# A product with two weight matrices, its seven-product form applied a second time and its weights read through a ring

## The chip, the cores and the metric

The kernel runs on one core of one Trainium2 chip. The metric is the device time of one execution in microseconds (us); lower is better. The core has a matrix engine (TensorE, in profiles PE, its weight loads PEld), three engines for element-wise work (VectorE or DVE, ScalarE or ACT, GpSimd or POOL), and SyncE (SP), which here issues all DMA transfers. Each engine runs its own instructions in program order and waits on semaphores for the others. Matmul results land in PSUM, in eight banks of 128 x 512 fp32 values[...].

## The reference

For 64 graphs of 256 nodes with 512 features, everything in fp32:

```python
def gcn(x, adj, W, b):
    return einsum('bnm,bmh->bnh', adj, einsum('bnf,fh->bnh', x, W)) + b

# layer 0: three graph convolutions, a residual and a layer norm
h = relu(gcn(x, adj, W1, b1)); h = relu(gcn(h, adj, W2, b2))
x = layernorm(x + gcn(h, adj, W3, b3))
# layer 1: a score for each node, a softmax over the nodes, a residual and a layer norm
q, k = split(x @ Wqk); v = x @ Wv
agg = einsum('bij,bjd->bid', adj, k * mask[:, :, None])
w = mask * einsum('bid,bid->bi', q, agg) / sqrt(512)
x = layernorm(x + softmax(w, axis=1)[:, :, None] * v)
```

The kernel forms M = Wq Wk^T once. Then the score of a node is the inner product of its row of x1 M with its row of A (x1 mask), where x1 is the result of layer 0. So layer 1 needs the product of x1 with two weight matrices, [Wv | M]: 256 x 512 times 512 x 1024 for each graph. The change is about this product.

## The kernel before

The graphs are worked in 32 pairs. The order on each engine is the order in which the code issues instructions (`manual_schedule`). For each pair there are three generators: `front` (F: layer 0 up to the third support), `back` (B: the last aggregation, the norm, the gather A x1, then `attention`, the double product with the scores) and `finish` (E: softmax, residual, norm, store). `run` interleaves front of pair i, back of pair i-1 and finish of pair i-2 by a string of letters written out by hand: `START` for the first round, `ORDER` for the 31 rounds after it, `END` for the round that has no front.

Products with 2 x 2 blocks are done with seven block products in place of eight. The helper `seven` issues them in the order 1, 7, 6, 2, 5, 3, 4 on three PSUM banks x, v and y, with a `yield` after each. Product 1 goes to x, is copied to SBUF by ScalarE (t1), then 6 is added in x and copied (u), then 5 is added and copied (q), then 3 is added and x holds block C12. Product 7 goes to v; VectorE forms C22 = v + q; then 4 is added in v and VectorE forms C21 = v + u. Product 2 goes to y and VectorE forms C11 = y + t1. So product 6 waits for the copy of t1, 5 for that of u, 3 for that of q, and 4 for VectorE's C22. The sums of the left operand are made by `a_sums` (four instructions, on GpSimd in the steady part), those of the right one by `b_sums`.

`front` runs three `support`s (four matmuls of 256 columns for each of the seven products) and two `aggregate`s (four steps of four matmuls). During the third support it issues on GpSimd the sums of the adjacency (`adj_sums`), the addition of b3 to x (`x<-x,b3b`, four instructions) and the `a_sums` of the next pair's input. `load_x`, `load_xT`, `load_adj` are DMA transfers on SP.

`back` writes the transposed x1 through DRAM (`via`) and back into `x1T`; GpSimd forms the sums S from it. Then `attention(g)` runs for each of the two graphs: seven products of two matmuls with 512 columns each (L451), the node halves and the feature halves of x1 against the blocks of [Wv | M], whose sums `mv` stay in SBUF for the whole kernel. The Wv part gives `v`; the M part is multiplied with the gathered rows `gt` and summed by `score` (VectorE). In the last round (`end`) the attention of the first graph is interleaved with the gather, and that of the second with the finish of the first.

An instruction of the program that multiplies fp32 operands shows as two instructions in the profile.

Of the kernel before, what the change touches and what calls it, by code (L numbers as in the profile page):

```python
# [19 lines left out]
@with_exitstack  # L20
def gcn_then_graph_attention(ctx: ExitStack, tc: tile.TileContext, xT, xN, adjT, mask, W1, b1, W2, b2, W3, b3,
                             WqT, WkT, Wv, out):

# [35 lines left out]
    def add(o, a, b):  # L61
        nc.vector.tensor_tensor(o, a, b, op=OP.add)  # L62
# [34 lines left out]

    def shaped(shape):
        t = tmp()
        return t.rearrange("p (a b) -> p a b", a=shape[1]) if len(shape) == 3 else t  # L100

    def seven(mm, shape, c11, c12, c21, c22, plus=None):

# [87 lines left out]
    eps = const.tile([P, 1], FP, name="eps")  # L191
    nc.vector.memset(eps, EPS)

    mv = {}

    def make_m():

        wq = pool.tile([P, DC, D], FP, name="wqT", tag="r", bufs=1)
        qk = [[wq[:, d] for d in range(DC)],
              [pool.tile([P, D], FP, name="wkT", tag="T", bufs=4) for _ in range(DC)]]  # L200
        for d in range(DC):
            for t, w in ((qk[0][d], WqT), (qk[1][d], WkT)):
                nc.sync.dma_start(t, w[d * P:(d + 1) * P, :])
        m = [pool.tile([P, 2, D], FP, name="m0", tag="v", bufs=2), const.tile([P, 2, D], FP, name="m1")]
        v0 = const.tile([P, 2, D], FP, name="v0")
        nc.sync.dma_start(v0, Wv[:HD].rearrange("(c p) f -> p c f", p=P))
        v1 = const.tile([P, 2, D], FP, name="v1")
        nc.sync.dma_start(v1, Wv[HD:].rearrange("(c p) f -> p c f", p=P))
        yield
        for f in range(DC):  # L210
            pt = bank((P, D))
            for d in range(DC):
                for j in range(DC):
                    nc.tensor.matmul(pt[:, j * P:(j + 1) * P], lhsT=qk[0][d][:, f * P:(f + 1) * P],  # L214
                                     rhs=qk[1][d][:, j * P:(j + 1) * P], start=(d == 0 and j == 0),
                                     stop=(d == DC - 1), skip_group_check=True)
            nc.scalar.copy(m[f // 2][:, f % 2, :], pt)
            yield
        ts = [const.tile([P, 2, D], FP, name=f"mv_{s}") for s in KEYS]
        b_sums((v0, m[0], v1, m[1]), ts, nc.vector)  # L220
        mv.update({1: v0, 2: v1, 3: m[1], 4: ts[3], 5: ts[0], 6: ts[1], 7: ts[2]})
        yield


    def a_sums(blk, eng=nc.gpsimd):

        S = [pool.tile([P, 2, G, P], FP, name="S", tag="S", bufs=11) for _ in range(4)]
        sub = OP.subtract  # L230

        def first():
            eng.tensor_tensor(S[2], blk(0, 0), blk(1, 0), op=sub)  # L233

        def rest():
            eng.tensor_tensor(S[0], blk(1, 0), blk(1, 1), op=OP.add)
            eng.tensor_tensor(S[1], S[0], blk(0, 0), op=sub)  # L237

        def last():
            eng.tensor_tensor(S[3], blk(0, 1), S[1], op=sub)  # L240
        return {1: blk(0, 0), 2: blk(0, 1), 4: blk(1, 1), 5: S[0], 6: S[1], 7: S[2], 3: S[3]}, first, rest, last

# [23 lines left out]
    def aggregate(C, aT, b):  # L266


        hT = [pool.tile([P, 2, G, N], FP, name="hT", tag="act", bufs=4) for _ in range(2)]
        src, first, rest, last = a_sums(lower_first(hT))  # L270
        for c in (2, 3, 0, 1):
            ps = bank()
# [21 lines left out]
        return {1: blk(0, 0), 2: blk(0, 1), 4: blk(1, 1), 5: S[:, 0], 6: S[:, 1], 7: S[:, 2], 3: S[:, 3]}  # L294

    def t_sums(B):
        Ts = [pool.tile([P, G, HD], FP, name="T", tag="T", bufs=4) for _ in range(4)]
        b_sums((B[0][0], B[0][1], B[1][0], B[1][1]), Ts, nc.gpsimd)
        return Ts

# [46 lines left out]
    def front(i, hT, src, aT):  # L347
        C = yield from support(src, wl[0])
        nxt = load_xT(i + 1) if i + 1 < NPAIR else None
        src, last = yield from aggregate(C, aT, bcol[0])  # L350
        C = yield from support(src, wl[1], last)
        src, last = yield from aggregate(C, aT, bcol[1])
        x = load_x(i)
        steps = support(src, wl[2], last)
        next(steps)
        yield
        next(steps)
        yield
        aS = adj_sums(aT)
        next(steps)  # L360
        yield
        for g in range(G):
            next(steps)
            for h in range(NH):
                padd(x[:, g, h, :], x[:, g, h, :], b3b)
            yield
        nS = None
        if nxt is not None:
            nS, first, rest, last = a_sums(lower_first(nxt))
            first()  # L370
            rest()
            last()
        C = yield from steps
        return C, aS, x, nxt, nS

    def back(i, C, aS, x, end):
# [63 lines left out]
        gt = pool.tile([P, NH, G, D], FP, name="gt", tag="gt", bufs=1)  # L440
        gb = lambda h, j: gt[:, h, :, j * HD:(j + 1) * HD]
        w = small.tile([P, NH, G], FP, name="w", bufs=2)
        vs = [None] * G

        def attention(g):
            b = i * G + g
            v = pool.tile([P, NH, D], FP, name="v", tag="v", bufs=2)

            def mm(n, ps, first):
                for c in range(2):  # L450
                    nc.tensor.matmul(ps, lhsT=src[n][:, c, g], rhs=mv[n][:, c], start=(first and c == 0),  # L451
                                     stop=(c == 1), skip_group_check=True)

            def score(y, h):
                nc.vector.scalar_tensor_tensor(y, y, mask_s[:, h, b:b + 1], gt[:, h, g, :], op0=OP.mult,
                                               op1=OP.mult, accum_out=w[:, h, g:g + 1])

            def c22(ps, t):
                add(t, ps, t)
                score(t, 1)  # L460
            vs[g] = v
            yield from seven(mm, (P, D), lambda y, t: add(v[:, 0, :], y, t), lambda x: score(x, 0),
                             lambda ps, t: add(v[:, 1, :], ps, t), c22)
        gather = adj_times(aS, xmb, Ts, lambda y, t: add(gb(0, 0), y, t), lambda x: nc.scalar.copy(gb(0, 1), x),
                           lambda v, t: add(gb(1, 0), v, t), lambda v, t: add(gb(1, 1), v, t))
        src, first, rest, last = a_sums(x1b, nc.vector if end else nc.gpsimd)
        if end:
            first()
            rest()
            last()  # L470
            one = attention(0)
            for k in "GMGMGMGMGGGMMM":
                next(gather if k == "G" else one)
                yield
            for _ in gather:
                pass
            for _ in one:
                pass
            tail = finish(i, (r, vs, w), [0])
            for _ in attention(1):  # L480
                next(tail, None)
                yield
            for _ in tail:
                pass
            for _ in finish(i, (r, vs, w), [1]):
                pass
            return
        for _ in range(4):
            next(gather)
            yield  # L490
        first()
        rest()
        last()
        yield from gather
        if i + 2 < NPAIR:
            aTs[i + 2] = load_adj(i + 2)
        for g in range(G):
            yield from attention(g)
        return r, vs, w

    def finish(i, prev, gs=range(G)):

        r, vs, w = prev
        n = len(gs)
        sm = softmax_rows(w, gs)
        yield
        s = softmax_cols(sm, gs)
        for k, g in enumerate(gs):
            for h in range(NH):
                nc.vector.scalar_tensor_tensor(vs[g][:, h, :], vs[g][:, h, :], s[:, h, k:k + 1], r[:, g, h, :],  # L510
                                               op0=OP.mult, op1=OP.add)
        yield
        st = small.tile([P, NH, n, 6], FP, name="st")
        mvt = small.tile([P, NH, n, 2], FP, name="mvt")
        for k, g in enumerate(gs):
            for h in range(NH):
                nc.vector.bn_stats(st[:, h, k], vs[g][:, h, :])  # L517
                yield
        for k in range(n):
            for h in range(NH):  # L520
# [2 lines left out]
        yield  # L523
        for k, g in enumerate(gs):
            for h in range(NH):
                nc.scalar.activation(vs[g][:, h, :], vs[g][:, h, :], AF.Identity, scale=rs[:, h, k:k + 1],  # L526
                                     bias=nb[:, h, k:k + 1])
                yield
            nc.sync.dma_start(out[i, :, g * NH * D:(g + 1) * NH * D].rearrange("p (h f) -> p h f", h=NH), vs[g])


    ORDER = ("F E F" + " B F" + " B F E" * 2 + " B B E F E F" + " B F E" + " B F B F F B B F F" +
             " B F B F B F E B B E F F" + " B F E B F E" + " B F E B F E B B F B F B F B" + " B F B F B B F B F B F B")
    START = "F" * 4 + "B" + "F" * 12 + "B" + "F" * 6 + "B FF B FFF B F B F"
    END = "E B B B E" + "B" * 5 + "B E" * 10

    def run(order, **gens):
# [15 lines left out]
    for i in range(NPAIR + 1):  # L553
# [14 lines left out]
        if i < NPAIR:  # L568
            C, aS, x, xTs, xS = res["F"]
            state = (C, aS, x)  # L570


# [33 lines left out]
```

## Time and profile before

| | |
|---|---|
| median of 3 runs | 2839.57 us (2838.18 to 2839.74) |
| the profiled execution | 2837.91 us, its span 2836.1 us |
| granted TensorE clock | 0.998 |
| DMA | 191.00 MB, mean 67 GB/s; SP's queue busy 21.1% of the 16 engines' span |
| chain, largest lines | L254 (support) 41%, L451 (attention) 27%, L275 (aggregate) 16%, L307 (gather and last aggregation) 13% |

A group in the profile reads: line, engine, operation, output<-inputs, shapes, count | busy time in us, mean time of one in ns | idle time of the engine just before these instructions, and who ended it. In a timeline a row begins with start and duration in us and may end with [idle before <-releaser]. Matmuls are pipelined, so the durations of neighbours overlap; the cost of one is the distance of the starts.

### The profile page before, as it was taken

The page shows a single profiled execution, that of the slowest core. Times are in us where ns is not written, and L with a number is a line of the kernel's source. Part 1 is how long each engine was busy: PE and PEld are TensorE (multiplying, and loading weights), DVE is VectorE, ACT ScalarE, POOL GpSimd, SP SyncE. Part 2 cuts the span into 40 slices and gives each one's busy share as a digit, 9 for nine tenths or more (in the row PEclk, how much of TensorE's full clock was granted, in tenths as well). Part 3 has the DMA queues.
Part 4 walks back from the last instruction along what each step waited for, and adds up shares of the span by engine and source line. Part 5 has one row for each costly group of instructions (what it writes and reads, how often), then busy time and mean ns, then how long its engine had stood idle before and what let it go on. Part 6 is the DMA issues. An engine that isn't in the chain of part 4 may idle for free.

```text
span 2836.1 us, 29920 instructions
## 1 busy us (share of the span) xinstructions
PE 2810.0 (99%) x11344; PEld 2191.4 (77%) x11344; DVE 1120.9 (40%) x2326; ACT 945.3 (33%) x1517; POOL 1437.5 (51%) x1122
## 2 busy tenths in 40 slices
PE   9999999999999999999999999999999999999997
PEld 8887778877778877787777788777887777877774
DVE  2444334443344443344433444333444334443335
ACT  2333233332333332333323333323333233333333
POOL 4545455445555455554555554556545455445551
PEclk9999999999999999999999999999999999999999
DMA  4211222211222112222122221122221222211210
GB/s 153 67 60 42 65 80 82 82 42 55 67 82 82 54 44 67 82 82 73 44 63 67 82 82 45 53 67 82 82 64 49 67 67 82 82 45 52 67 60 30
DMA packets 63086, 191.00 MB, mean 67 GB/s; under 512 B 5728, under 2 KB 8928, under 8 KB 54880
## 3 DMA queue, kind: packets, MB, share of 16 engines
q1 hardware_dynamic: 62944, 189.10, 21.1%
q8 instruction: 90, 1.47, 0.2%
q14 instruction: 52, 0.43, 0.1%
HBM read 123.02 MB, written 66.06 MB: 67 GB/s over the span
## 4 chain that ended last, share of the span: by engine, by line
PE 97%; DVE 1%; DMA 1%; ACT 1%; issue 0%; SPq 0%; POOL 0%; ACTq 0%; DVEq 0%; POOLq 0%
PE ps L254 41%; PE ps L451 27%; PE ps L275 16%; PE ps L307 13%; PE ps L214 1%; DMA aT<-in_adjT 0%; PE ps L341 0%; PE ps L326 0%; DMA mask_t<-in_mask 0%; ACT v L526 0%; SPq L149 0%; DVE st L517 0%; POOL tmp L65 0%; DMA out<-v 0%; DVE st L388 0%
## 5 line engine op out<-in xcount | busy, mean ns | idle before, releaser
L254 PE MATMUL ps<-w_T,S 128*128 128x256 f32 x2304 | 546.9, 380 | 2.3 <-POOL S L237 1.5
L254 PEld LDWEIGHTS ps<-w_T,S 128*128 128x128 f32 x2304 | 432.5, 190 | 106.6 <-issue 52.1
L275 PE MATMUL ps<-aT,sup 128*128 128x256 f32 x2048 | 472.7, 379 | 0.0
L275 PEld LDWEIGHTS ps<-aT,sup 128*128 128x128 f32 x2048 | 389.1, 190 | 76.1 <-issue 22.2
L62 DVE TENSOR_TENSOR sup<-ps,tmp 128x512 f32<-128x512 f32 x288 | 198.4, 689 | 526.8 <-PE ps L254 338.4
L451 PE MATMUL ps<-mv_T,S 128*128 128x512 f32 x768 | 361.0, 592 | 0.0
L65 POOL TENSOR_TENSOR tmp<-tmp,x 128x512 f32<-128x512 f32 x96 | 120.5, 1270 | 418.8 <-ACT tmp L126 242.3
L278 ACT ACTIVATE hT<-ps,b 128x512 f32<-128x512 f32 x256 | 175.4, 685 | 377.1 <-PE ps L275 377.1
L62 DVE TENSOR_TENSOR v<-ps,tmp 128x512 f32<-128x512 f32 x128 | 88.5, 692 | 535.5 <-PE ps L451 531.8
L118 ACT COPY tmp<-ps 128x512 f32<-128x512 f32 x224 | 131.3, 586 | 486.3 <-PE ps L254 223.4
L109 ACT COPY tmp<-ps 128x512 f32<-128x512 f32 x224 | 130.7, 583 | 418.0 <-PE ps L254 283.7
L126 ACT COPY tmp<-ps 128x512 f32<-128x512 f32 x224 | 130.7, 583 | 339.0 <-PE ps L254 221.4
L254 PE MATMUL ps<-w,hT 128*128 128x256 f32 x1024 | 241.9, 379 | 0.0
L451 PE MATMUL ps<-v,x1T 128*128 128x512 f32 x512 | 240.6, 592 | 0.0
L254 PEld LDWEIGHTS ps<-w,hT 128*128 128x128 f32 x1024 | 194.5, 190 | 46.3 <-issue 14.8
L451 PEld LDWEIGHTS ps<-mv_T,S 128*128 128x128 f32 x768 | 145.8, 190 | 102.1 <-issue 92.3
L233 POOL TENSOR_TENSOR S<-x1T 128x512 f32<-128x512 f32 x31 | 67.9, 2190 | 275.7 <-DMA x1T<-via 275.7
L307 PE MATMUL ps<-T,aS 128*128 128x256 f32 x768 | 200.3, 383 | 0.3 <-ACT tmp L109 0.3
L451 PEld LDWEIGHTS ps<-v,x1T 128*128 128x128 f32 x512 | 146.2, 290 | 69.3 <-issue 17.7
L233 POOL TENSOR_TENSOR S<-hT 128x512 f32<-128x512 f32 x64 | 81.2, 1269 | 220.5 <-ACT hT L278 220.5
L254 PE MATMUL ps<-w,S 128*128 128x256 f32 x768 | 181.5, 379 | 0.7 <-issue 0.7
L93 POOL TENSOR_TENSOR T<-sup 128x512 f32<-128x512 f32 x32 | 41.0, 1281 | 272.8 <-ACT sup L256 272.8
(109 smaller groups left out, 4179.9 us busy)
## 6 DMA issues: line engine op xcount, KB each, us to landing
x<-in_xN SPq DMA_DIRECT2D x32, 1024.0 KB, 5.7
out<-v SPq DMA_DIRECT2D x64, 512.0 KB, 3.3
xT<-in_xT SPq DMA_DIRECT2D x31, 1024.0 KB, 4.9
via<-tr SPq DMA_DIRECT2D x31, 1024.0 KB, 4.3
x1T<-via SPq DMA_DIRECT2D x124, 256.0 KB, 4.7
aT<-in_adjT SPq DMA_DIRECT2D x32, 512.0 KB, 4.3
w<-in_W SPq DMA_DIRECT2D x9, 256.0 KB, 5.2
xT<-in_xT SPq DMA_DIRECT2D x2, 512.0 KB, 5.1
```

The source lines that it names most:

```text
L62: nc.vector.tensor_tensor(o, a, b, op=OP.add)
L65: nc.gpsimd.tensor_tensor(o, a, b, op=op)
L93: eng.tensor_tensor(Ts[2], B[3], B[1], op=sub)
L109: nc.scalar.copy(t1, x)
L118: nc.scalar.copy(u, x)
L126: nc.scalar.copy(q, x)
L233: eng.tensor_tensor(S[2], blk(0, 0), blk(1, 0), op=sub)
L254: nc.tensor.matmul(ps[:, g], lhsT=src[n][:, c, g], rhs=w[n][:, c], start=(first and g == 0 and c == 0), stop=(g == G - 1 and c == 1), skip ...
L275: nc.tensor.matmul(ps[:, g], lhsT=C[k][c // 2][:, g, (c % 2) * P:(c % 2 + 1) * P], rhs=aT[:, k, g], start=(g == 0 and k == 0), stop=(g == ...
L278: nc.scalar.activation(hT[c // 2][:, c % 2], ps, AF.Relu, bias=b[:, c:c + 1])
L307: nc.tensor.matmul(ps[:, g], lhsT=aS[n][:, g], rhs=mov[n][:, g], start=(first and g == 0), stop=(g == G - 1), skip_group_check=True)
L451: nc.tensor.matmul(ps, lhsT=src[n][:, c, g], rhs=mv[n][:, c], start=(first and c == 0), stop=(c == 1), skip_group_check=True)
```

## The change

The seven block products of the double product (the outer ones) are each again split 2 x 2 and done with seven products (the inner ones). In an inner product the rows are the two graphs of the pair, the contraction is 2 x 128 features and the columns are 2 x 256. That gives 7 x 7 = 49 matmuls of 128 x 128 by 128 x 256 for a pair, where 28 matmuls of 128 x 128 by 128 x 512 stood (two graphs, seven products, two matmuls each).

The outer products run in four groups: a = (1, 2), b = (6, 5), c = (7, 4), d = (3). A step of a, b or c does one inner product for two outer products into one bank; a step of d does one. The groups a and b alternate step by step, then follow c and d. With them come:

- `attention` is one generator for the pair. ScalarE copies three blocks of x1T to Z and VectorE makes the four sums of Z; GpSimd makes the inner sums I in two groups of four. The first inner sums of x1T by GpSimd (S) go.
- Each group collects its blocks in R (a and c in the buffer T, b and d in that of x1T), and VectorE combines the groups with six additions of 1024 columns; d adds to what R holds, three of these additions on GpSimd. Both graphs' scores follow c and d.
- `make_m` forms the 49 weight operands in round 0 and stores them in DRAM (`w_dram`). A ring of 7 SBUF buffers of 256 KB is filled by `fetch`: after each step the transfer for the seventh step after it is issued on SP.
- Fewer buffers: S 11 to 7, hT 4 to 2, T one tile of four parts, v one tile.
- In `front`, the next pair's sums are issued in steps 2 and 5 of the third support, and the additions of b3 in steps 3 and 4. `ORDER` and `START` are rewritten. In the last round only the first steps of a and b stand in the gather, and the finish of both graphs follows the whole product.

```diff
-    mv = {}
+    OUTER = ((1, 2), (6, 5), (7, 4), (3,))
+    INNER = (1, 7, 6, 2, 5, 3, 4)
+    STEPS = "ab" * 7 + "c" * 7 + "d" * 7
+    place = {n: k for k, n in enumerate(n for q in OUTER for n in q)}
+    w_dram = [dram.tile([P, 7, len(q), HD], FP, name=f"mv_{k}", bufs=1) for k, q in enumerate(OUTER)]
...
+    RING = 7
+    ring = {}
+    def fetch(k):
+        if k < NPAIR * len(uses):
+            q, n = uses[k % len(uses)]
+            t = pool.tile([P, 2, HD], FP, name="ring", bufs=RING)
+            nc.sync.dma_start(t[:, :len(OUTER[q])], w_dram[q][:, n])
+            ring[k] = t
...
+        for q, outer in enumerate(OUTER):
+            w = pool.tile([P, 7, len(outer), HD], FP, name="w7", tag="ZI"[q % 2], bufs=1)
+            for k, n in enumerate(outer):
+                blk = [B[n][:, c, j * HD:(j + 1) * HD] for c in range(2) for j in range(2)]
+                for i, b in ((1, blk[0]), (2, blk[2]), (3, blk[3])):
+                    nc.scalar.copy(w[:, at[i], k], b)
+                b_sums(blk, [w[:, at[i], k] for i in (5, 6, 7, 4)], nc.vector)
+                yield
+            nc.sync.dma_start(w_dram[q], w)
+        for k in range(RING):
+            fetch(k)
...
         steps = support(src, wl[2], last)
...
+        for n in range(6):
             next(steps)
-            for h in range(NH):
-                padd(x[:, g, h, :], x[:, g, h, :], b3b)
+            if n == 1:
+                aS = adj_sums(aT)
+            if n == 2 and nxt is not None:
+                nS, first, rest, last = a_sums(lower_first(nxt))
+                first()
+                rest()
+            if n in (3, 4):
+                for h in range(NH):
+                    padd(x[:, n - 3, h, :], x[:, n - 3, h, :], b3b)
+            if n == 5 and nxt is not None:
+                last()
             yield
...
-                    nc.tensor.matmul(ps, lhsT=src[n][:, c, g], rhs=mv[n][:, c], start=(first and c == 0),
-                                     stop=(c == 1), skip_group_check=True)
...
+    def attention(i, x1b, gt, w):
+        Z = pool.tile([P, 7, 4, P], FP, name="Z", tag="Z", bufs=1)
+        I = pool.tile([P, 4, 7, P], FP, name="I", tag="I", bufs=1)
...
+        for n, b in ((1, x1b(0, 0)), (2, x1b(0, 1)), (4, x1b(1, 1))):
+            nc.scalar.copy(z(n), b)
+        for o, a, b, op in ((z(5), x1b(1, 0), x1b(1, 1), OP.add), (z(6), z(5), z(1), sub), (z(7), z(1), x1b(1, 0), sub),
+                            (z(3), z(2), z(6), sub)):
+            nc.vector.tensor_tensor(o, a, b, op=op)
+        for a, b in ((0, 4), (4, 7)):
+            padd(I[:, 2, a:b], Z[:, a:b, 0], Z[:, a:b, 1], sub)
+            padd(I[:, 0, a:b], Z[:, a:b, 1], Z[:, a:b, 3])
+            padd(I[:, 1, a:b], I[:, 0, a:b], Z[:, a:b, 0], sub)
+            padd(I[:, 3, a:b], Z[:, a:b, 2], I[:, 1, a:b], sub)
...
+            def mm(n, ps, first):
+                wt = ring.pop(at[0])
+                for k, o in enumerate(outer):
+                    nc.tensor.matmul(ps[:, k], lhsT=left[n](place[o]), rhs=wt[:, k], start=(first and k == 0),
+                                     stop=(k == len(outer) - 1), skip_group_check=True)
+                fetch(at[0] + RING)
+                at[0] += 1
...
+            if count[k] == 7:
+                if k == "a":
+                    add(v[:, :, 0], flat(R["a"][:, 0]), flat(R["a"][:, 1]))
+                elif k == "b":
+                    U, V = R["b"][:, 0], R["b"][:, 1]
+                    add(U, U, R["a"][:, 0])
+                    add(V, V, U)
+                elif k == "c":
+                    P7, P4 = R["c"][:, 0], R["c"][:, 1]
+                    add(P4, P4, U)
+                    add(v[:, :, 1], flat(P7), flat(P4))
+                    add(P7, P7, V)
+                    score(P7, 1)
+                else:
+                    score(V, 0)
+            yield
+        return v
...
-    ORDER = ("F E F" + " B F" + " B F E" * 2 + " B B E F E F" + " B F E" + " B F B F F B B F F" +
-             " B F B F B F E B B E F F" + " B F E B F E" + " B F E B F E B B F B F B F B" + " B F B F B B F B F B F B")
-    START = "F" * 4 + "B" + "F" * 12 + "B" + "F" * 6 + "B FF B FFF B F B F"
+    ORDER = ("F F E" + " B F" + " B F E" * 2 + " B B E F E F" + " B F E" + " B F B F F B B F F" +
+             " B F B F B F E B B E F F" + " B F E B E" + " B E F E F" + " BB BB BB BB F BB BB BB" +
+             " B B F B B F B F B B F B B F B B F B F B B")
+    START = "F" * 4 + "B" + "F" * 12 + "B" + "F" * 5 + "B F B F B B" + "F B" * 6
...
+    for _ in finish(NPAIR - 1, prev):
+        pass
```

## What the change does to the time, predicted before it was measured

> **What bounds the kernel now.** I read the shares of the engines first, then the chain of waits, then the groups of instructions with shapes kept apart, and last the timelines of one pair of graphs in the steady part, of pair 0 and of the end.
>
> ```profile
> span 2836.1 us, 29920 instructions
> PE 2810.0 (99%) x11344; PEld 2191.4 (77%) x11344; DVE 1120.9 (40%) x2326; ACT 945.3 (33%) x1517; POOL 1437.5 (51%) x1122
> ...
> PE 97%; DVE 1%; DMA 1%; ACT 1%; issue 0%; SPq 0%; POOL 0%; ACTq 0%; DVEq 0%; POOLq 0%
> ...
> L451 PE MATMUL ps<-mv_T,S 128*128 128x512 f32 x768 | 361.0, 592 | 0.0
> ...
> L65 POOL TENSOR_TENSOR x<-x,b3b 128x512 f32<-128x512 f32 x128 | 172.3, 1376 | 0.0
> ```
>
> TensorE is the path: 97% of the chain; apart from its own weight loads, which overlap its matmuls, no engine is over 51%. "Idle before" is zero at L451, so in the steady part nothing makes TensorE wait. A mean of 592 ns is a latency; the cost is the distance of starts, from the timeline of TensorE:
>
> ```profile
> 1075.99 1.89 PE L275 MATMUL ps<-aT,sup 128*128 128x256 f32 x8
> 1077.71 1.88 PE L451 MATMUL ps<-v,x1T 128*128 128x512 f32 x4
> 1079.43 1.89 PE L275 MATMUL ps<-aT,sup 128*128 128x256 f32 x8
> 1081.16 1.88 PE L451 MATMUL ps<-mv_T,S 128*128 128x512 f32 x4
> ```
>
> Four instructions of 512 columns take 1.717 us (429 ns each), eight of 256 take 1.725 us (216 ns each): the cost goes with columns. Pairs start 86.9 us apart (the softmax's reduction at 1032.53 and 1119.43).
>
> Two further views price what the change adds, VectorE and GpSimd in pair 0:
>
> ```profile
> 73.62 1.22 DVE L94 TENSOR_TENSOR mv_T<-m,v 128x1024 f32<-128x1024 f32 x1
> 74.87 2.17 DVE L95 TENSOR_TENSOR mv_T<-m,mv_T 128x1024 f32<-128x1024 f32 x1
> 77.07 2.17 DVE L96 TENSOR_TENSOR mv_T<-v,mv_T 128x1024 f32<-128x1024 f32 x1
> ...
> 74.25 1.71 POOL L93 TENSOR_TENSOR T<-sup 128x512 f32<-128x512 f32 x1 [4.22 <-ACT sup L256]
> 75.92 2.25 POOL L94 TENSOR_TENSOR T<-sup 128x512 f32<-128x512 f32 x1
> ```
>
> An addition of two SBUF operands of 1024 columns takes 1.12 us from start to start alone, but 2.17 us beside a GpSimd one, and that one 2.25 in place of 1.27: each waits until the other has ended. And the end of the kernel, where one step follows another without cover:
>
> ```profile
> 2773.01 1.03 PE L307 MATMUL ps<-T,aS 128*128 128x256 f32 x4
> 2774.71 1.13 PE L307 MATMUL ps<-sup,aS 128*128 128x256 f32 x4 [0.68 <-ACT tmp L126]
> ```
>
> The step at 2773.01 occupies TensorE to 2773.88; the next, on the same bank, starts 0.83 us later. So the copy between two uses of a bank needs 0.83 us of other work.
>
> **What the Trainium skill says.** "SBUF — State Buffer", section "Who interferes with whom": a VectorE instruction with two SBUF inputs contends with a GpSimd instruction that reads SBUF, and the second to issue blocks until the first has finished; the lines above agree (1.12 to 2.17). "TensorE: Matmul & The Clock Gate", table at its head: the queues of ScalarE, VectorE and GpSimd are strict FIFO, so what stands behind a blocked instruction waits too; the trace shows ScalarE's and VectorE's starts in program order. "DMA: Bandwidth & Descriptors", section "Specifications", limits HBM to about 358 GB/s for a core; here 189.10 MB took 21.1% of the span, 316 GB/s while busy, and the measurement counts.
>
> **The change part by part**, for one pair in the steady part.
>
> TensorE. Removed: 2 graphs x 7 products x 2 matmuls, two instructions each, 56 x 429 ns = 24.04 us. Added: 49 matmuls of 256 columns, 98 x 216 = 21.17. Gain 2.85 us a pair; the weights now come from contiguous Z and I (190 ns loads, where x1T took 290), hidden either way under 216. Over 31 pairs -88 us. What counts is whether TensorE stays fed. In totals it does: VectorE gains 3 PSUM additions (0.6), 4 half ones (0.35), 4 sums of Z (0.65) and 6 of 1024 columns (1.12), 12.5 us on 34.3 of 84; ScalarE some 7 us on 29; GpSimd loses 7.2 us (S<-x1T) and gains 8.8 (eight sums of I) and 2.1 (three half additions in d). No engine becomes the bound by its sum; the order decides.
>
> I lay out TensorE's new order from a1 (t = 0, 49.0 us into the pair, the place where the trace has 1079.43). A step of a, b, c takes 0.865, of d 0.43, of the next pair's support or aggregation 1.725. So: a1 0, b1 .87, a7 1.7, b7 2.6, a6 3.46, b6, a2, b2 6.1, aggregation 6.9, a5 8.65 ... b4 13.0, c1 13.8, c7, F0 15.6, c6, c2, F1 19.0, c5, F2, c3 23.4, c4 24.2-25.1, F3, d1 26.8, d7, F4 27.7, d6, d2, F5 30.3, d5 32.0, F6 32.45, d3, d4, next pair at 35.0. (F0 to F6: the seven products of the third support.)
>
> Banks. The tightest uses, a5 to a3 and b5 to b3, have one step of 0.865 between, against 0.83: no stall, at most 0.1.
>
> Early wait (a6). x1T lands at t = -4.4: GpSimd's S<-x1T waits for it to 1075.06. ScalarE has before the three copies to Z a relu (to -3.4) and two normalisations (0.71 each), so Z1 is there at -1.3 and Z2 at -0.6, Z6 on VectorE at -0.6. GpSimd's first I then starts behind Z7 (0), ends at 1.3 (a7 needs it at 1.7), the second waits for VectorE's Z3 and ends at 3.1, the third, which a6 needs, at 4.35. Stall 0.9. Bounds: 0 if the lock is not met (third I at 3.5), 2.0 if the stride of x1T slows the copies as it slows GpSimd (2.19 against 1.27). Behind a6 all of TensorE is queued.
>
> Late wait (F6). F6 adds into the bank that VectorE must first have read for C22 of the same support. That addition stands in VectorE's queue behind the end of c: after c4 (25.1, plus 0.26 to VectorE's start as at L62 now) come one PSUM addition 0.6, three of 1024 columns 3.36, two scores of 0.7, then C11 and C22 of the support 1.3: 32.05 without contention, and F6 loses nothing (0.4 spare). But GpSimd gets d's first half addition at 27.9 (d1's end, then ScalarE's copy), and behind it the last two of x+b3b (1.25 each, two SBUF operands), all ready. Alternating as in pair 0 these three go between the last five SBUF instructions of VectorE: +0.7, +1.25, +1.25, so F6 starts at 35.15. Stall 2.7. Bounds: 0, and 5.8 if all five wait for a GpSimd instruction of 1.25 (x late from its DMA, so all four of x+b3b fall there). Behind F6: d3, d4 and the next pair. Its softmax transposes at 3.45 us need the scores of d, then some 0.5 earlier: nothing added.
>
> SP and DMA. 28 ring transfers of 256 or 128 KB add 6.4 MB to a pair that moves 6.0 now. In the a/b phase one of 256 KB is wanted each 0.865 us (303 GB/s), but each is issued seven steps ahead, 5.2 to 6.9 us; 512 KB land in 3.3 to 4.3 us now, 1024 in 4.9 to 5.7, so 256 KB need about 3.5 (estimate from these). SP's issue is 0.35 to 0.43, under 0.865. Past them must go aT and the second out<-v; before x<-in_xN stand the fetches up to c7, so x comes at t = 16 and lands near 22, used at 23. Price taken: 0; bounds 0 and 2.5 (rival 3).
>
> Fewer buffers (hT, S, T, v at half): their readers end before the reuse in this order (S's last sum waits for F4, 29.4, and isn't needed before the next pair). 0.
>
> End. No support lies beside c and d, both graphs are normalised after all products. From the first product of the second gather (2787.4), by the durations that the end of the trace shows: gather with a1 and b1 10 us (with its waits of 0.97 and 1.16), the other twelve a/b steps 10.4, c 6.9 (seven steps and one 0.83), VectorE's end of c 5.6, d's sums and scores 3.3, softmax 3.7, its application 2.7, statistics and normalisation 6.8, last landing 3.7: 2840.5, +4 us (0 to +12).
>
> Start. 21 copies and 32 additions that build the ring's source lie beside the last support of pair 0, where VectorE and GpSimd meet again: +6 (0 to +15).
>
> Sum against the profiled execution (2837.91 us, 1.8 around its span): 31 x (0.9 + 2.7 - 2.85) = +23, +4, +6: 2871. The median shown is 1.7 above the profiled one: 2873.
>
> **The rivals.** (1) The cover holds (faster): GpSimd's three additions miss the end of c, F6 starts on time. For it: GpSimd is at 51%, and VectorE's own sum leaves 0.4 us. Against it: d1's addition becomes ready in the midst of these sums. 31 x (0.9 - 2.85) + 10 = -50: 2789. It decides once F6's stall is under 1.6 us (2.85 - 0.9 - 10/31). (2) A tie: stalls near 2.5 us in all, as with one GpSimd addition fewer in the way: 2840. (3) The ring is late: at 200 GB/s (aT and out in between) nine fetches need 11.8 us where they have about 11, with the landing some 2.5 us too late, over 31 pairs +78 on the forecast: 2951. Against it: 316 GB/s while busy.
>
> **How the numbers follow.** The lock (2873): 0.52. Rival 1: 0.30; rival 2: 0.08; rival 3: 0.10. Slower by over 0.2% (some 6 us, about what a measurement can tell) 0.62, same 0.08, faster 0.30. The likeliest's own range, stalls of 2.7 to 5.0 us in all with the bounds of start and end, is 2845 to 2925; with rival 1 it reaches down to 2785, and leaves out rival 3 and the ends of the bounds.
>
> **What would show it.** Matmuls from the ring 216 ns apart: the gain. Idle of TensorE before the support's last product, released by VectorE's sup: the late wait, about 2.7 us x 31; before the ring,I products, released by GpSimd: the early one. VectorE's 1024 additions at 2 us rather than 1.22 would prove the lock; at 1.22, and no idle at F6, the forecast is wrong and rival 1 right. Idle released by the ring's DMA is rival 3.

## The result, and the profile after

The changed kernel takes 2929.88 us (median of 4 runs, 2924.93 to 2940.91) against 2839.55 us of the kernel before, measured beside it: 1.0325 times as long, with a 95% interval of 1.0295 to 1.0354. The profiled execution took 2928.85 us. Forecast were 2873 us, with a range of 2785 to 2925: the direction is right, the size is not, and the time lies outside the range.

From the page of the changed kernel: span, engines, the chain of waits by engine, groups of instructions (out<-in, count, busy us, mean ns of one, idle us just before them and what ended it), and the last line a DMA issue with its median time to landing.

```profile
span 2927.0 us, 36919 instructions
...
PE 2776.6 (95%) x12684; PEld 2377.3 (81%) x12684; DVE 1774.5 (61%) x2888; ACT 1167.2 (40%) x1917; POOL 1756.3 (60%) x1350
...
PE 74%; DVE 11%; POOL 5%; ACT 4%; issue 3%; DMA 2%; SPq 0%; ACTq 0%; DVEq 0%
...
L520 PE MATMUL ps<-ring,I 128*128 128x256 f32 x1792 | 455.3, 385 | 32.7 <-POOL I L68 31.5
...
L65 DVE TENSOR_TENSOR R<-R 128x1024 f32<-128x1024 f32 x128 | 232.3, 1815 | 9.2 <-DVE R L65 0.5
L68 POOL TENSOR_TENSOR x<-x,b3b 128x512 f32<-128x512 f32 x128 | 207.5, 1642 | 15.4 <-DMA x<-in_xN 9.7
...
L289 PE MATMUL ps<-w_T,hT 128*128 128x256 f32 x512 | 141.1, 424 | 78.0 <-DVE sup L65 78.0
...
ring<-mv SPq DMA_DIRECT2D x672, 256.0 KB, 3.2
```

TensorE's share of the chain fell from 97% to 74%. Most of its idle time in the steady part stands at two places. 78.0 us come before the product with w_T and hT that waits for VectorE's sup: the support's last product, F6. 32.7 us come before a product of the ring with I, a6, which waits for GpSimd's third sum of I. A ring transfer lands in 3.2 us, and none of TensorE's groups waits for one.

One steady pair on TensorE's timeline (start us, duration us, operation, in brackets the idle before it and what ended it):

```profile
1118.76 1.99 PE L520 MATMUL ps<-ring,I 128*128 128x256 f32 x8
1121.77 1.99 PE L520 MATMUL ps<-ring,I 128*128 128x256 f32 x8 [1.02 <-POOL I L68]
...
1150.61 0.59 PE L520 MATMUL ps<-ring,I 128*128 128x256 f32 x2
1153.65 1.99 PE L289 MATMUL ps<-w_T,hT 128*128 128x256 f32 x8 [2.44 <-DVE sup L65]
```

The first two starts are 3.01 us apart where eight instructions need 1.73: a6 costs 1.28 us. F6 starts 3.04 us after an instruction pair that needs 0.43: 2.61 us. What holds F6 is on VectorE's timeline,

```profile
1144.56 1.56 DVE L65 TENSOR_TENSOR R<-R 128x1024 f32<-128x1024 f32 x1
1146.15 1.22 DVE L65 TENSOR_TENSOR v<-R 128x1024 f32<-128x1024 f32 x1
1147.41 1.63 DVE L65 TENSOR_TENSOR R<-R 128x1024 f32<-128x1024 f32 x1
1149.08 1.64 DVE L538 SCALAR_TENSOR_TENSOR R<-R,mask_s,gt 128x512 f32<-128x512 f32 x1
1150.65 1.74 DVE L538 SCALAR_TENSOR_TENSOR R<-R,mask_s,gt 128x512 f32<-128x512 f32 x1
1152.32 1.28 DVE L65 TENSOR_TENSOR sup<-ps,tmp 128x512 f32<-128x512 f32 x2
```

and on GpSimd's beside it:

```profile
1146.37 1.59 POOL L68 TENSOR_TENSOR tmp<-tmp,R 128x256 f32<-128x256 f32 x1 [1.33 <-PE ps L520]
1147.92 3.92 POOL L68 TENSOR_TENSOR x<-x,b3b 128x512 f32<-128x512 f32 x2
```

The three sums and two scores at the end of c stand in VectorE's queue ahead of the support's two additions. While GpSimd adds b3 (two in 3.92 us, where two take 2.49 undisturbed), a sum takes 1.63 instead of 1.22 and a score 1.7 instead of 0.75. That is the late wait as the prediction described it.

What the prediction did not have is in the durations of F6 itself. Two pairs of the changed kernel, again TensorE's timeline:

```profile
261.79 3.63 PE L289 MATMUL ps<-w_T,hT 128*128 128x256 f32 x8 [2.12 <-DVE sup L65]
...
439.81 1.99 PE L289 MATMUL ps<-w_T,hT 128*128 128x256 f32 x8 [2.12 <-DVE sup L65]
```

The same eight instructions after the same idle take 1.64 us longer in the first. The windows view gives, for two stretches around the start of each, the length, the busy time (and count) of PE, PEld, DVE, ACT, POOL, then the granted TensorE clock (then DMA share and GB/s):

```profile
258.31:261.73 3.42, 1.36 (x7) 0.85 (x5) 3.42 (x7) 0.86 (x2) 3.42 (x3) 1.00 0.67 210
261.73:265.14 3.41, 3.35 (x8) 2.73 (x9) 0.76 (x3) 0.00 (x0) 3.41 (x4) 0.50 0.03 11
435.81:439.22 3.41, 1.88 (x9) 1.32 (x7) 3.41 (x6) 0.86 (x2) 3.41 (x3) 1.00 0.66 171
439.22:442.63 3.41, 2.83 (x13) 2.52 (x14) 2.08 (x5) 0.00 (x0) 3.41 (x5) 1.00 0.17 65
```

The first F6 runs at a granted clock of 0.50, the second at 1.00. After the idle, the clock came back at half speed in 9 of the 31 pairs (counted over the trace: an F6 of over 2.9 us). So the pairs are 88.2 us apart, and about every third 89.8 or more, against 86.9 before. From the first softmax transposes to those of the last round, 30 pairs, this adds 60.9 us; the start, with one pair's product in it, added 16.6 (first transposes at 179.74 instead of 163.11) and the end 13.4 (81.1 us from the last round's transposes on, instead of 67.7). The sum is 90.9, the difference of the spans.

### The profile page after: what moved, and what is told of

Read it like the earlier page. It is cut to its first block, busy times and chain, and to the rows that moved or that the text cites. A ratio compares the mean times of both kernels' runs of the same rounds, so it can differ in the third digit from the quotient of the medians.

```text
span 2927.0 us, 36919 instructions
## 1 busy us (share of the span) xinstructions
PE 2776.6 (95%) x12684; PEld 2377.3 (81%) x12684; DVE 1774.5 (61%) x2888; ACT 1167.2 (40%) x1917; POOL 1756.3 (60%) x1350
## 3 DMA queue, kind: packets, MB, share of 16 engines
HBM read 328.54 MB, written 72.48 MB: 137 GB/s over the span
## 4 chain that ended last, share of the span: by engine, by line
PE 74%; DVE 11%; POOL 5%; ACT 4%; issue 3%; DMA 2%; SPq 0%; ACTq 0%; DVEq 0%
PE ps L289 32%; PE ps L520 18%; PE ps L343 12%; PE ps L310 11%; POOL I L68 5%; DVE R L65 4%; DVE R L538 2%; ACT Z L500 2%; ACT v L593 2%; DVE v L65 1%; DVE sup L65 1%; DMA x1T<-via 1%; DMA via<-tr 1%; DVE tr L463 1%; PE ps L235 0%
## 5 line engine op out<-in xcount | busy, mean ns | idle before, releaser
L65 DVE TENSOR_TENSOR R<-ps,tmp 128x512 f32<-128x512 f32 (+1 forms) x384 | 238.1, 621 | 416.7 <-PE ps L520 288.7
L520 PE MATMUL ps<-ring,I 128*128 128x256 f32 x1792 | 455.3, 385 | 32.7 <-POOL I L68 31.5
L520 PEld LDWEIGHTS ps<-ring,I 128*128 128x128 f32 x1792 | 332.5, 191 | 110.8 <-POOL I L68 55.8
L68 POOL TENSOR_TENSOR I<-Z 128x384 f32<-128x384 f32 (+1 forms) x128 | 172.1, 1364 | 401.4 <-ACT Z L500 400.7
L520 PE MATMUL ps<-ring,Z 128*128 128x256 f32 x1344 | 332.9, 380 | 4.3 <-DVE R L65 4.0
L114 ACT COPY tmp<-ps 128x512 f32<-128x512 f32 (+1 forms) x288 | 158.1, 561 | 429.7 <-PE ps L289 278.5
L123 ACT COPY tmp<-ps 128x512 f32<-128x512 f32 (+1 forms) x288 | 162.1, 563 | 408.2 <-PE ps L343 192.0
L520 PEld LDWEIGHTS ps<-ring,Z 128*128 128x128 f32 x1344 | 255.5, 190 | 40.3 <-DVE R L65 4.4
L131 ACT COPY tmp<-ps 128x512 f32<-128x512 f32 (+1 forms) x288 | 161.5, 561 | 277.1 <-PE ps L289 130.2
L65 DVE TENSOR_TENSOR R<-R 128x1024 f32<-128x1024 f32 x128 | 232.3, 1815 | 9.2 <-DVE R L65 0.5
L68 POOL TENSOR_TENSOR x<-x,b3b 128x512 f32<-128x512 f32 x128 | 207.5, 1642 | 15.4 <-DMA x<-in_xN 9.7
L289 PE MATMUL ps<-w_T,hT 128*128 128x256 f32 x512 | 141.1, 424 | 78.0 <-DVE sup L65 78.0
```

Of the source, the lines that this page charges most:

```text
L68: nc.gpsimd.tensor_tensor(o, a, b, op=op)
L114: nc.scalar.copy(t1, x)
L123: nc.scalar.copy(u, x)
L131: nc.scalar.copy(q, x)
L289: nc.tensor.matmul(ps[:, g], lhsT=src[n][:, c, g], rhs=w[n][:, c], start=(first and g == 0 and c == 0), stop=(g == G - 1 and c == 1), skip ...
L520: nc.tensor.matmul(ps[:, k], lhsT=left[n](place[o]), rhs=wt[:, k], start=(first and k == 0), stop=(k == len(outer) - 1), skip_group_check= ...
```

## Experiments

All times below are beside the kernel before on the same chip (2839 to 2840 us). A time without a range is one run. Single runs of the changed kernel itself lie up to 16 us apart, so differences below that are read from the traces instead.

### Is it the lock, the ring, ScalarE's queue, or the clock?

**The later half of the additions of b3 left out** (`front`):

```diff
-            if n in (3, 4):
+            if n == 3:
```

> Part left out: the last two additions of b3 to x on GpSimd in each pair (step 4 of the third support). Nothing else moves. Lock theory: the end of c on VectorE meets two GpSimd instructions fewer, so the idle before the support's last product (2.1 to 2.4 us in the changed kernel) falls by about two times 1.25 less what the next GpSimd instruction, which moves up, takes back: to 0 to 1.2 us; the device time falls by 30 to 75 us from 2930. Queue theory (VectorE's own instructions are too many, the lock adds little): the idle stays at 2 us and the time at 2925 to 2940. Ring theory (transfers late): unchanged too.

Measured: 2881.6 us, 48 less. The idle before F6 fell from 2.27 us a pair (the mean of all) to 1.20, and F6 never ran at half clock. 31 x 1.07 = 33 us of idle and 9 x 1.64 = 15 us of slow products make up the 48. Of VectorE's two scores ahead of F6, which took 1.64 and 1.74 us, the second takes 0.74 here (at 1130.09 us). Two GpSimd additions that TensorE never waits for directly cost that much because they lie beside VectorE's sums.

**The ring filled once, with no further weight transfers** (the same seven tiles serve again):

```diff
-                fetch(at[0] + RING)
+                k = at[0]
+                if k + RING < NPAIR * len(uses):
+                    ring[k + RING] = wt
```

> Part left out: the ring is filled once with seven operands, which all later steps use again; no transfer of weights after round 0 (6.4 MB a pair less). Ring theory: TensorE no longer waits, 2850 or below. Lock theory and queue theory: both waits stay, the early one at 1.0 us and the late one at 2.1 us, pairs 88.2 us apart or up to 0.5 less (the next pair's x can land earlier, the early out has fewer transfers behind it): 2905 to 2930.

Measured: 2925.2 us, both waits as before (F6 2.13 us a pair, half clock in 9 pairs). HBM reads fell from 328.54 to 124.85 MB and the time did not follow: the ring costs nothing that shows.

**ScalarE's copies to Z ahead of two normalisations:**

```diff
-" B F E B E" + " B E F E F"
+" B F B" + " B E E F E E F"
```

> Only the hand-written order changes: two normalisations of the pair before (ScalarE, 0.71 us each) are issued after the three copies of x1T to Z in place of before them. If the early wait comes from ScalarE's queue, as the prediction has it, Z is there 1.4 us earlier and the idle before the third inner product (1.02 us, with its surroundings 1.4) goes: pairs 1.2 to 1.5 us closer, device time 2880 to 2895. If it is GpSimd's own time from x1T's landing (x1T, then sums), or the landing itself, the idle stays at 1 us. The late wait stays in all theories.

Measured: 2925.85 us, not the 2880 to 2895 of the theory. The idle before a6 fell only from 1.02 to 0.73 us: the first two sums of I, beside VectorE's sums of Z, took 3.62 us here and 3.42 in the changed kernel, where two undisturbed ones take 2.5. Pairs at full clock did become shorter (87.6 to 88.2 us), but half clock came in 17 pairs instead of 9. A shorter pair gave no shorter kernel.

**TensorE kept busy while it waits for F6:** 9 products of the identity ahead of it, whose results nobody uses.

```diff
+        warm(9)
         C = yield from steps
```

> Nine matmuls of 128 columns (18 instructions, 2.1 us, result unused) are added before the support's last product in every pair, where TensorE is idle for 2.1 us anyway. Clock theory: in some nine of thirty pairs that product runs at half speed (3.6 us in place of 1.8) because TensorE's clock was lowered during the idle time; with the gap filled no pair is 1.6 us longer than the others, the granted clock is back at 0.998 from 0.987, and the device time falls by 10 to 20 us although work was added. If the long pairs have another cause (a refresh, a late transfer), they stay and the time is the same or higher by up to 20 us.

Measured: 2911.57 us, 18 less with more work. TensorE's timeline of this kernel, at the pair shown above:

```profile
259.42 2.17 PE L173 MATMUL ps<-ident 128*128 128x128 f32 x18
261.71 1.99 PE L289 MATMUL ps<-w_T,hT 128*128 128x256 f32 x8
```

The idle is filled, F6 takes 1.99 us, and every pair is 88.2 to 88.7 us long. So the long pairs were the clock, and what brought it down was the idle.

### Does each wait cost its own length?

**VectorE's end of c taken apart,** so that the support's C22 comes earlier:

```diff
                     add(v[:, :, 1], flat(P7), flat(P4))
-                    add(P7, P7, V)
-                    score(P7, 1)
                 else:
                     score(V, 0)
+            elif k == "d" and count[k] == 1:
+                add(P7, P7, V)
+            elif k == "d" and count[k] == 3:
+                score(P7, 1)
...
-            if n == 5 and nxt is not None:
-                last()
             yield
         C = yield from steps
+        if nxt is not None:
+            last()
```

> VectorE's tail at the end of c is taken apart: of its three sums of 1024 columns and two scores, the last sum goes to d's first step and the two scores to d's third, and GpSimd's last sum for the next pair's first layer goes behind the support. Nothing is left out. If the support's last product waits because VectorE's C22 stands behind this tail, its idle of 2.1 to 2.4 us goes, the half-clock products that follow it go with it, and the pair falls from 88.7 on average to about 86: 2840 to 2855 us. If it waits for something else (the bank, ScalarE's copy), the idle stays and the time is within 10 us of 2930.

Measured: 2841.03 us. The pair fell to 85.9 us in nearly every case, and the idle before F6 from 78.0 us to 7.8 in the whole run, with the early wait unchanged at 1.02. The two moves, VectorE's sums and scores and GpSimd's last sum, were worth 89 us together: 70 of idle (31 x 2.27), 15 of half clock, and a few elsewhere. What each is worth alone was not tried.

**One aggregation between a7 and a6,** to cover the early wait alone:

```diff
-" BB BB BB BB F BB BB BB"
+" BB BB F BB BB BB BB BB"
```

> The last aggregation of the second layer goes from behind a2, b2 to ahead of a6, b6 (1.72 us of TensorE work between a7, b7 and a6, b6); nothing is left out. If the early wait is only GpSimd's third sum of I being about 1.0 us late, its idle goes from every pair and the pair falls by 1.0 to 1.3 us, so 2890 to 2900 us, the late wait being unchanged. If GpSimd's sums are late because they compete with VectorE, and TensorE's products only move that lateness on (the layer's own sums follow on GpSimd), the time stays within 8 us of 2930.

Measured: 2983.14 us, 53 more, outside both expectations. The groups of this kernel:

```profile
L520 PE MATMUL ps<-ring,I 128*128 128x256 f32 x1792 | 460.2, 388 | 1.3 <-issue 0.7 <-ACT tmp L131 0.5
...
L289 PE MATMUL ps<-w_T,hT 128*128 128x256 f32 x512 | 177.0, 507 | 121.7 <-DVE sup L65 121.7
```

The early wait is gone (32.7 to 1.3 us), and the late one grew by more (78.0 to 121.7). Its cause is on VectorE's timeline:

```profile
1070.18 1.91 DVE L65 TENSOR_TENSOR R<-R 128x1024 f32<-128x1024 f32 x1
1072.12 1.67 DVE L65 TENSOR_TENSOR v<-R 128x1024 f32<-128x1024 f32 x1
1073.83 2.17 DVE L65 TENSOR_TENSOR R<-R 128x1024 f32<-128x1024 f32 x1
```

The three sums took 1.56, 1.22 and 1.63 us; moved against GpSimd's queue, all three now meet one of its additions, 1.34 us more. After this idle, 3.7 us on average, F6 ran at half clock in all 31 pairs.

**Both edits together** (e5 and e7):

> The edits of e5 and e7 together. If the two waits and the half clock after the late one are all that a steady pair lost, the pair falls to 84.05 us plus at most 0.5 and the kernel to 2790 to 2805 us, faster than the kernel before (2840) by the 2.85 us a pair of TensorE work that the change removes. If removing them only brings up a next wait (ring, banks, VectorE), the pair stays above 85.5 and the time above 2835.

Measured: 2837.85 us, 86.0 us a pair: the second expectation. F6 starts on time, a6 too, and TensorE waits at two new places of the same pair:

```profile
1117.36 0.70 PE L520 MATMUL ps<-ring,Z 128*128 128x256 f32 x2 [0.45 <-DVE R L65]
...
1122.05 0.38 PE L362 MATMUL ps<-ident,w 128*2 128x128 f32 x2 [0.54 <-DVE R L538]
```

Counted from start to start these two, d4 and the softmax's transposes, cost 0.62 + 0.70 = 1.32 us, about as much as the 1.28 that a6 had cost. Whether the equal size is more than chance was not tried.

**Scores behind d4, the softmax's transposes later:**

```diff
-    ORDER = ("F F E" + " B F" + " B F E" * 2 + " B B E F E F" + " B F E" + " B F B F F B B F F" +
+    ORDER = ("F F" + " B F E" + " B F E" * 2 + " B B E F E F" + " B F E" + " B F B F F B B F F" +
...
                 else:
                     score(V, 0)
+                    score(P7, 1)
-            elif k == "d" and count[k] == 3:
-                score(P7, 1)
```

> e8 (86.0 us a pair) still waits 0.62 us before d4 and 0.70 us before the softmax's transposes, both for VectorE. Here both pairs of scores come behind d4, and the transposes of the softmax one step of the gather and one of the support later (2.59 us). Nothing is left out. If these two waits are the last of the pair, it falls to 84.6 to 84.9 us and the kernel to 2790 to 2800 us: the 2.85 us a pair of TensorE work come back in full. If VectorE's queue carries the wait on to a next place, the pair stays at 85.5 or above and the time above 2820.

Measured: 2834.44 us, 85.8 us a pair. Again the wait went on, to the next thing that the softmax must deliver:

```profile
1127.06 0.25 PE L377 MATMUL ps<-ident,e 2*128 2x2 f32 x2 [1.14 <-DVE e L370]
```

**The column transposes later too,** by one gather step and one support step (e14), or by the gather step alone (e15). Both contain e11's edits and the start of e12, below; the first new line is e14's, the second e15's.

```diff
-"F F" + " B F E" + " B F E" * 2 + " B B E F E F"
+"F F" + " B F E" + " B F B F E E" + " B B E F E F"
+"F F" + " B F E" + " B F B E F E" + " B B E F E F"
```

> In e13 the only wait left in a steady pair (85.8 us) is 1.30 us before the softmax's column transposes, for VectorE's scaling of e, behind an activation table load of 1.28 us on ScalarE. Here these transposes come one more gather step and one more support step later (2.59 us); nothing is left out. If a pair holds no other bound, it falls to 84.5 to 84.8 us and the kernel to 2790 to 2800 us, ratio 0.983 to 0.986. If the four VectorE instructions that apply the softmax (2.74 us), now later, hold up the support's additions, a new wait comes up at the first layer's last product and the time stays above 2815.

> As e14, but the column transposes come only one gather step (0.86 us) later. If only the chain of the softmax counts, 0.4 us of the 1.3 stay: 84.9 to 85.1 us a pair, 2802 to 2810 us. If the application of the softmax on VectorE is the next bound, this one is as fast as e14 or faster.

Measured: e14 2801.59 us (2801.19 to 2802.75), 0.987 of the kernel before, interval 0.9853 to 0.9886; e15 2805.59 us, 0.9884, interval 0.9869 to 0.9899. The pairs are 84.8 and 85.0 us apart, as the first theory had it; e14's time is 1.6 us above its range. From the page of e14:

```profile
span 2799.4 us, 36905 instructions
...
PE 2752.5 (98%) x12684; PEld 2366.5 (85%) x12684; DVE 1715.1 (61%) x2888; ACT 1165.8 (42%) x1917; POOL 1746.8 (62%) x1350
...
PE 96%; DVE 2%; DMA 1%; ACT 1%; POOL 0%; issue 0%; SPq 0%; ACTq 0%; DVEq 0%; POOLq 0%
```

TensorE is the chain again, with the same 12684 instructions and nearly the same load on the other engines as in the changed kernel. No work was taken out between 2929.88 and 2801.59 us: the order differs, and in pair 0 the buffers of the build.

### The start

**Pair 0 with the build of the ring's source earlier** (its order alone):

```diff
-"B" + "F" * 12 + "B" + "F" * 5 + "B F B F B B" + "F B" * 6
+"B" + "F" * 8 + "B FF B FF B FF B B" + "F B" * 3 + "F B B" * 2
```

> Only the order of pair 0 differs from the changed kernel: the four products of m and the sums that build the ring's source are spread over the second layer instead of lying beside the last support. If the 16.6 us of the start are VectorE's queue (support additions behind the build), the first pair's end falls from 179.7 to 163 to 167 and the time to 2913 to 2918. If they are the transfers or the build's length itself, less than 5 us come back.

Measured: 2935.75 us, first transposes at 182.87, 3 us later. ScalarE stood 10.54 us at its copies for a staging buffer still being written to DRAM, with the support's evictions behind it, and TensorE 10.35 us for one of those.

**Four staging buffers** (Z, I, the seven ring tiles, the buffer of x1T), the first two blocks built from Wv before m is complete:

```diff
-            w = pool.tile([P, 7, len(outer), HD], FP, name="w7", tag="ZI"[q % 2], bufs=1)
+    stage = [pool.tile([P, 7, 2, HD], FP, name="w7", tag=t, bufs=1) for t in "ZI"]
...
+    stage.append([pool.tile([P, 2, HD], FP, name="ring", bufs=RING) for _ in range(7)])
+    w = pool.tile([P, 7, 1, HD], FP, name="w7s", tag="x1T", bufs=1)
...
+"F" * 8 + "B FF BB FF BB FF BB" + "F B" * 6
```

> Only pair 0 differs from the changed kernel: the ring's source is built in four buffers instead of two, so that no copy waits for a buffer to be written to DRAM, its first two blocks before m is complete and the rest beside the second layer's aggregation. If e9 came out no better because ScalarE and VectorE stood behind the buffers' write (10.5 us in its trace, with the support's evictions queued behind), the first pair's end falls from 179.7 to 163 to 168 and the time by 10 to 16 us, to 2914 to 2920. If the length of VectorE's work is the cause, it stays above 174 and the time within 6 us of 2930.

Measured: 2926.67 us, first transposes at 178.06, only 1.7 us earlier. The idle at the same product shrank, and the clock fell after it all the same. The changed kernel's line and, from e12, the line in its place:

```profile
83.71 3.78 PE L289 MATMUL ps<-w_T,hT 128*128 128x256 f32 x8 [7.67 <-DVE sup L65]
```

```profile
80.06 3.78 PE L305 MATMUL ps<-w_T,hT 128*128 128x256 f32 x8 [3.64 <-DVE sup L65]
```

Smaller waits for GpSimd and ScalarE (1.44, 0.77 and 0.78 us) took part of the rest. So the second expectation holds: the buffers were not the main cost. The additions of the build and those of the support share VectorE's queue whatever the order; what of the 16.6 us could be had back was not settled.

**Start and steady part together** (e11 and e12):

> The edits of e11 and of e12 together. If steady part and start are separate costs, the gains add: 2775 to 2790 us, a ratio of 0.977 to 0.983 to the kernel before, with only the end (13 us) left against the forecast of TensorE's work alone. If e11 finds a next wait, 2810 to 2825.

Measured: 2831.49 us (2830.77 to 2834.14), 0.9972, interval 0.9962 to 0.9982; 6 us above what the second case allowed, since the start gave less. Its first transposes come 1.7 us before e11's, and e11's wait stands in every pair.

## Why the prediction was wrong, by its own steps

**TensorE's gain, 2.85 us a pair: right.** e14's pair is 84.8 us where 86.9 - 2.85 = 84.05 was worked out. The 0.75 between them are small gaps, from start to start, where one kind of product follows another: eleven of 0.07 to 0.21 us in the pair of e14 that starts at 1046.7 us, 1.26 us in all, against four with 0.48 us in one of the kernel before. In the one before a7 (0.16 us) the weights are GpSimd's first sums of I; what makes the others was not followed up.

**Early wait, 0.9 taken, 1.28 measured.** Of the bounds (0 to 2.0) the upper one's reason applied: a copy from the strided x1T took 1.0 us (three in 3.02), while at the end, where x1T is not strided so, three took 1.66. The working laid the lateness on ScalarE's queue and GpSimd's sums; e3, which took 1.4 us out of that queue, left 0.73 of the 1.02 us of idle. So the queue is the smaller part. That the sums of I are slow for VectorE's sums of Z beside them is read from their durations; no run took the two apart.

**Late wait, 2.7 taken, 2.45 measured** (2.27 of idle on average, and 0.18 more from start to start): mechanism and size right, shown by e1 and e5. A sum of 1024 columns was counted at 1.12 us undisturbed; the starts in the kernel before are 1.15 apart (72.47 and 73.62 us), and here such a sum took 1.22.

**Everything else between products at 0, the banks at most at 0.1: too low.** In the changed kernel about 0.65 us a pair are left when the other parts are taken off (60.9 + 85.5 us of lost gain, less 30 x 1.28, 30 x 2.45 and 15, divided by 30). They have the size of the small gaps above, which had no term. Whether any of them are the banks is not shown.

**No term for the clock: the step that was missing.** "A stall costs its length" stands behind the whole sum. 9 pairs cost 1.64 us more, 15 us. The Trainium skill, "TensorE: Matmul & The Clock Gate", Part 1, "What's actually happening", tells of a half-rate state after at least one idle window of about 3.4 us, free-running. The two speeds agree with this trace (a granted clock of 0.50 from 796.4 to 800.0 us, within such a product, and 1.00 in others). So does the window: the 15 half-clock stretches in the changed kernel's clock record all start a whole number of times 3.413 us apart (12.55, 80.82, 261.73, 527.97 and so on to 2907.05). The threshold doesn't: in no case was a window before F6 wholly idle. In the nine pairs hit, 2.06 us or more of the idle before F6 lay within one window, as in 258.31:261.73 above; in the 22 others it was 1.86 at most, as an idle of the same length is split by the border at 439.22. In all seven kernels with this wait (the changed one, e1, e2, e3, e7, e9, e12) the bound is the same: 2.01 us or more in all 87 pairs that were hit, less in the 130 that were not. So the place of the idle against these windows decides. A pair of 88.20 us is 0.55 short of 26 windows, the idle moves by 0.55 us against them from pair to pair, and about every third pair is hit. In e1 no more than 1.84 us ever lay in one window; in e7 it was 2.01 or more in every pair.

**Start, +6 taken (bound 15), 16.6 measured; end, +4 taken (bound 12), 13.4 measured.** For their size these two terms are the most mis-sized, 19 of the 58 us. In the start, the additions were priced as lying beside the support; they stand in front of it in one queue, F6's counterpart waited 7.67 us and then ran at half clock. In the end, the working priced the second gather with its first ring products at 10 us; they took 15.7 (2865.93 to 2881.62). ScalarE's timeline of the changed kernel shows why,

```profile
2873.81 0.30 ACT L350 ACTIVATE sd<-mvt,eps 128x4 f32<-128x4 f32 x1 [3.82 <-DVE mvt L588]
2874.01 0.57 ACT L123 COPY tmp<-ps 128x512 f32<-128x512 f32 x1
```

and TensorE's what it cost:

```profile
2874.63 1.13 PE L343 MATMUL ps<-T,aS 128*128 128x256 f32 x4 [2.54 <-ACT tmp L123]
```

ScalarE waited in its queue for the previous pair's statistics, and the gather's eviction stood behind. A second wait for ScalarE (2.29 us, at 2878.05) follows. Neither was in the sum, though the text had named the queues as strict. The two waits are 4.8 us where the 10 us held 2.1, and after the second eight matmul instructions of the gather ran at a granted clock of 0.50, some 1.8 us more. That is 4.5 of the 5.7; the rest of the end was not followed up.

**Ring and fewer buffers at 0: right for the ring** (e2). The buffers were not tested alone; e14, with the same ones, leaves only the 0.75 us a pair above unexplained by TensorE's work.

**The sum.** 30 x 1.28 us a pair too little (2.03 measured, 0.75 forecast) is 38 us: small gaps 20, clock 15, early wait 11, less 8 for the late wait. The start is 9.9 (16.6 less 6 and less the 0.75 forecast for the pair in it), the end 9.4. Together 58, and the profiled times differ by 58 (2928.85 and 2871). Of the rivals, the first (cover holds, 2789) and the second (tie, 2840) are out by the 78.0 us before F6, the third (ring late, 2951) by e2, though its time came nearest. The 0.62 on slower was borne out. The stalls came to 4.88 us a pair (2.85 and 2.03), within the 2.7 to 5.0 of the likeliest case. Its upper end was added up too low: 31 x (5.0 - 2.85) us with both bounds, 15 and 12, gives 2933 us, not 2925.

**The two waits as independent terms: wrong, though it didn't hurt this sum.** e7 removed one and the other grew. e8 and e11 removed both and about 1.3 us came up at the next place: in e8 behind VectorE's queue, in e11 at the end of the softmax's chain, in which VectorE itself waits (3.08 us for the transposes and 1.86 for ScalarE in e13). Only when the last of these places was moved (e14) did the time follow.

## What to carry to other kernels

A saving on the engine that bounds a kernel is only had if every result that it reads is ready earlier as well: follow the queues and chains behind it to the last reader, and expect a wait that you take away to reappear there until the last one is covered. Price a stall by more than its length: here 2.1 us of idle on TensorE cost another 1.6 us of half clock wherever 2.0 us of it lay in one window of 3.41 us (9 pairs of 31), and unneeded products in the gap won 18 us. When work goes into a queue, put it behind what the critical engine waits for, not only beside idle time.

## What the runs showed of the hardware

- TensorE's clock was halved for 3.41 us, or a multiple of it, on a grid of 3.413 us, after a grid window with 2.01 us or more of F6's idle in it (87 pairs in seven kernels; 130 pairs with less kept the full clock). The eight instructions of F6 then took up to 3.78 instead of 1.99 us.
- ScalarE's copy of 512 columns out of the strided x1T takes 1.0 us; where x1T lies in another order, at the end, 0.55. VectorE's addition takes 1.03 instead of 0.69 us.
- A ring transfer of 256 KB landed in a median 3.2 us (3.5 had been estimated), with 137 GB/s of HBM traffic on average over the span.
- The exponential of the softmax brings a table load of 1.28 us on ScalarE; in e13 it ran from 1122.24 to 1123.52 us, while the maxima that the exponential needs were ready at 1122.26: all of it on the path of the column transposes. The Trainium skill, "ScalarE: Activation LUTs", "What ACT_TABLE_LOAD costs", gives about 1283 ns for the load; the trace agrees.
